# A planner that values work by its place in the run, and a second layer's setup that it can see

## Chip, cores and metric

The kernel runs on one core of one Trainium2 chip. The metric is the device time of one execution in microseconds; before the change it is 4598.14 us, the median of three runs (4592.67 to 4598.62).

## What is computed

Two layers over an fp32 tensor of 8 images, 192 channels, 64 x 64 pixels. Weights are fp32 throughout.

```python
# layer 0: windowed attention that keeps 16 keys, then an MLP
shortcut = layer_norm(xs); q, k, v = windows(shortcut) @ qkv_w.T          # 8x8 windows, 6 heads of 32
attn = l2n(q) @ l2n(k).T * temperature
attn = where(attn >= top_k(attn, 16)[..., -1:], attn, -100)
x2 = shortcut + proj(softmax(attn + rpb) @ v)
x  = x2 + fc2(gelu(fc1(layer_norm(x2))))
# layer 1: a filter in frequency space, then an MLP
xf = fft2(layer_norm(x) * n1_g + n1_b)                                    # over the 64 x 64 image
x  = x + ifft2(fc2(gelu(fc1([xf.real, xf.imag])))).real                   # 2 -> 16 -> 2
out = x + mlp2(gelu(mlp1(layer_norm(x))))                                 # 192 -> 768 -> 192
```

## The kernel before, in words

**Tiling.** Layer 0 works on bands of 8 rows (512 pixels): 8 bands an image, 64 in all. For each band, `front` transposes, normalizes and forms q, k and v; `attention` runs twice (once for each half of the windows); `back` projects, adds and runs the first MLP. Layer 1's filter works on groups of 16 channels: 12 groups an image, 96 in all. For each group, `forward` makes the first half of the transform (tiles `xf`, `fa`, `fz`), `pointwise` runs twice with its GELU (`fh`, `fo`), and `inverse` transforms back (`fb`, `fy`). It can begin when all 8 bands of an image have left layer 0. `leave` then runs the second MLP for each band, when all 12 groups of the image are done. In tile names, `_b` is the first MLP and `_d` the second: `mh_b`, `mh_d` are the products ahead of the GELU, `mo_b`, `mo_d` those behind it. `s` and `po` are attention's scores and its sums over values. From the second image on, attention weights go through DRAM to be turned (`tt`, `ar`, `at`, in `turned_by_dma`), and so do the MLPs' inputs (`lt`, `lr`, `hn`).

**Order.** Nothing in the order is written by hand, and no scheduler runs on the chip. Every task is a Python generator, and before each group of instructions it yields `op(engine, weight, ...)`: the engine, the time in units of 10 ns (the half of an MLP's second product has weight 390 and takes 3.90 us), the buffers it takes (`get`) and gives back (`put`), and what it waits for (`after`). `Plan.run` plays these through a model with five engine clocks. On each engine it takes, of the ops that could begin within 15 units, the one with the smallest key; the key is the begin time plus the task's `place` (360 units an image) plus noise. `Plan.search` (line 278) advances by 2000 units at a time: it tries 80 random noises to a horizon of 4000 units, rates each by the PE work in it plus 0.15 of the other engines' work, and keeps the first 2000 units of the best. `issue` then emits the instructions in that order, so each engine's queue has exactly the planned sequence. Semaphores hold the data dependences; a queue never overtakes.

**Modes.** TensorE's ops carry a mode name: `full` for 128-row products, `row64`, `row32`, `col32`, `s` and `v` for smaller arrangements of the array. The model charges 19 units for a change of mode on PE and 140 for a change of function on ACT (`CHANGE`, line 35).

**Buffers and arrivals.** `ARRIVES` (line 36) says how long after its end an op's result is seen by another engine: 28 units for PE, 18 for DVE, 15 for ACT, 11 for POOL, 265 for a DMA issued by SP. A buffer given back is free 150 units after an SP op and 15 after any other (line 268).

**Layer 1's setup.** `setup_layer1` (line 606) loads tables and weights through SP after the first attention half of band 0, in an op with no weight, so the plan sees no time on SP for it. The scale vector `n1g` comes through eight transfers whose source steps by four elements:

```python
src = bass.AP(n1t.tensor, n1t.offset + c * 2 * HC + k, [[0, 32], [4, 24], [1, 1]])
dst = n1g[32 * k : 32 * k + 32, 24 * c : 24 * c + 24]
nc.sync.dma_start(dst.unsqueeze(2), src)
```

Its DVE part waits for `("att", 0, 1, 1)`. `setup_mlp(1, ...)` (products `pf`, DVE scaling of `wmlp`) waits for `("att", 0, 5, 1)`.

Of the kernel before, what the change touches and what calls it, by code (L numbers as in the profile page):

```python
# [2 lines left out]

# [6 lines left out]
FP = mybir.dt.float32  # L10
# [6 lines left out]
C = 192  # L17
CA = 128
HC = 96
# [10 lines left out]
def op(engine, weight, mode=None, get="", put="", after=None, done=None, put_too=""):  # L30
    engines = ((engine, weight),) if isinstance(engine, str) else tuple(zip(engine, weight))
    return engines, mode, get.split(), (put + " " + put_too).split(), after, done
# [97 lines left out]
class Plan:  # L130
# [84 lines left out]
    def run(self, until, noise=None):  # L215
        ops, clock, mode, units = self.ops, self.clock, self.mode, self.units
        at, front, place, ready = self.at, self.front, self.place, self.ready
        while ready:
            found = {}
            for task, (number, begins) in ready.items():  # L220
                a = front[task]
                if a is not None and at[a] <= at[task]:
                    continue
                _, kind, counts, put, _, _ = ops[number]
                free = 0
                for name, n in counts:
                    u = units[name]
                    if len(u) < n:
                        break
                    if u[n - 1] > free:  # L230
                        free = u[n - 1]
                else:
                    best = None
                    for engine, weight, begin in begins:
                        if clock[engine] > begin:
                            begin = clock[engine]
                        if free > begin:
                            begin = free
                        change = kind and mode[engine] and kind != mode[engine]
                        cost = CHANGE[engine] if change else 0  # L240
                        end = begin + cost + weight + (40 if engine == "dve" else 0)
                        if best is None or end < best[0]:
                            best = end, engine, begin, cost, weight
                    _, engine, begin, cost, weight = best
                    key = begin + cost + place[task] - (100 if "ps" in put else 0)
                    if noise:
                        key += noise(number)
                    found.setdefault(engine, []).append((key, task, begin, cost, weight, number))
            if not found:
                return False  # L250
            chosen = None
            for engine, entries in found.items():
                first = min(e[2] + e[3] for e in entries) + 15
                e = min(e for e in entries if e[2] <= first)
                if chosen is None or (e[2], e[0]) < chosen[0]:
                    chosen = (e[2], e[0]), engine, e
            _, engine, (_, task, begin, cost, weight, number) = chosen
            if begin >= until:
                return True
            _, kind, counts, put, _, _ = ops[number]  # L260
            for name, n in counts:
                del units[name][:n]
            begin += cost
            end = begin + weight
            clock[engine] = end
            mode[engine] = kind or mode[engine]
            for name in put:
                units[name].append(end + (150 if engine == "sp" else 15))
                units[name].sort()
            self.end[number], self.engine[number] = end, engine  # L270
            self.log.append((number, task, engine, begin, weight))
            del ready[task]
            for other in self.blocked.pop(number, ()):
                self.wake(other)
            self.step(task)
        return True

    def search(self, tries=80, step=2000, horizon=4000, spread=25):
        draw = random.Random(1)
        now = 0  # L280
        while self.ready:
            now = max(now, self.clock["pe"])
            kept, best = self.save(), None
            for k in range(tries):
                seed = draw.random()
                noise = drawn(seed, spread) if k else None
                if not self.run(now + horizon, noise):
                    self.restore(kept)
                    continue
                worth = 0  # L290
                for _, _, engine, begin, weight in self.log[kept[-1]:]:
                    part = min(weight, max(0, now + horizon - begin))
                    worth += part if engine == "pe" else 0.15 * part
                if not self.ready:
                    worth = 1e9 - max(self.clock.values())
                if best is None or worth > best[0]:
                    best = worth, seed if k else None
                self.restore(kept)
            seed = best[1]
            self.run(now + step, drawn(seed, spread) if seed is not None else None)  # L300
            now += step
        return [(self.names[task], engine, number) for number, task, engine, _, _ in self.log]


def drawn(seed, spread):
    draw, values = random.Random(seed), {}

    def noise(number):
        if number not in values:
            values[number] = draw.gauss(0, spread)  # L310
        return values[number]

    return noise
# [28 lines left out]
def program(ctx, tc, x, out, w):  # L342
    nc = tc.nc
# [114 lines left out]
    def load_mlp(name1, name2):  # L458
        w1, w2 = load_ab(name1, DFF), ctile(name2, [128, 6, 64 + C])
        nc.sync.dma_start(w2[:, :, 64:], w[name2].rearrange("(c p) f -> p c f", p=128))  # L460
        return w1, w2
# [107 lines left out]
    def setup_mlp(layer, weights, gain, offset, after):  # L569
        yield op("pe", 120, "full", get="ps", after=after)  # L570
        w1, w2 = weights()
        pf = psum(f"pf_{layer}")
        for f in range(6):
            times(pf[:, 0, f : f + 1], w1, slice(f * 128, f * 128 + 128), offset)
        yield op("dve", 30, put="ps")
        nc.vector.tensor_tensor(fcb[:, layer], fcb[:, layer], pf[:, 0, 0:6], ALU.add)
        for k in range(2):
            yield op("dve", 64)
            scale(w1[k : k + 1], gain[k : k + 1])
        yield op("dve", 45, done=("mlp", layer))  # L580
        nc.vector.tensor_copy(w2[:, :, 0:64], w2[:, :, C:])
# [22 lines left out]
    wmlp = []  # L604

    def setup_layer1():
        yield op("pool", 0, get="xf", after=[("att", 0, 0, 1)])
        for j, name in enumerate(("fcos", "fsin")):
            nc.sync.dma_start(
                fhalf[:, j], w[name].rearrange("p (c u) -> p c u", c=2)[:, :, 0:U]  # L610
# [1 line left out]
            for e in range(2):  # L612
                own = w[name][64 * e : 64 * e + 64]
                for c in range(2):
                    rows = 64 * c + 32 * e
                    nc.sync.dma_start(ihalf[j][rows : rows + 32], own[0:32])

        for t in range(4):
            row = 64 * (t % 2) + 32
            nc.sync.dma_start(ihalf[1][32 * t : 32 * t + 1], w["fcos"][row : row + 1])  # L620
        for k in range(4):
            src = w["fwd2"].rearrange("(a b k e) v -> k b a e v", a=2, k=4, e=2)[k]
            nc.sync.dma_start(frow[8 * k : 8 * k + 8], src)
        for c in range(1, 4):
            nc.sync.dma_start(frow[32 * c : 32 * c + 32], frow[0:32])
        inv1 = sb.tile([128, 128], FP, tag="xf", name="inv1", bufs=1)
        nc.sync.dma_start(inv1, w["inv1"])
        sel1 = load("sel1", [128, 2, 8])
        sel2 = load("sel2", [128, 2, 16])
        aw1 = load("aw1", [128, 16])  # L630
        aw2 = load("aw2", [128, 2])
        nc.sync.dma_start(ab, w["ab"])
        n1t = w["n1"]
        for c in range(2):
            for k in range(4):
                src = bass.AP(
                    n1t.tensor, n1t.offset + c * 2 * HC + k, [[0, 32], [4, 24], [1, 1]]
                )
                dst = n1g[32 * k : 32 * k + 32, 24 * c : 24 * c + 24]
                nc.sync.dma_start(dst.unsqueeze(2), src)  # L640
            nc.sync.dma_start(n1b2[:, c, :], w["n1"][c : c + 1, 1, :])
        yield op("dve", 120, after=[("att", 0, 1, 1)])
        for e in range(2):
            for a in range(2):
                of = inv1[:, a * HW : (a + 1) * HW].rearrange("p (b k e) -> p e k b", k=4, e=2)
# [26 lines left out]
        yield op("dve", 50, done="layer1")  # L672
        nc.vector.tensor_scalar(dc, ab[0:1, 1:2], float(HW), None, ALU.mult)
        nc.vector.tensor_scalar(n1b2, n1b2, float(HW), None, ALU.mult)
        wmlp.extend(load_mlp("wmlp1", "wmlp2"))


# [784 lines left out]
    def leave(b, j):  # L1462
# [49 lines left out]
        ([(setup_rpb(), -0.1)], 1),  # L1512
        ([(setup_mlp(0, lambda: (wfc1, wfc2), vec(G2), vec(B2), ["rows", (None, 3000)]), -0.5)], 1),
        ([(setup_layer1(), 0.2)], 1),
        ([(setup_mlp(1, lambda: wmlp, *layer1, ["layer1", ("att", 0, 5, 1)]), 0.2)], 1),
        ([(front(b, i), at_band(b, i, -.12)) for b, i in bands], 1),
        ([(attention(b, i, hb), at_band(b, i, -.085)) for b, i in bands for hb in range(2)], 3),
        ([(back(b, i), at_band(b, i, .215)) for b, i in bands], 2),
# [86 lines left out]
```

## Time and profile before

| | |
|---|---|
| median of three runs | 4598.14 us |
| the profiled execution: its own time, and its span | 4606.84 us, 4605.0 us |
| TensorE clock granted, mean | 0.984 |
| busy: PE, its weight loads, DVE, ACT, POOL | 4377.8, 3470.0, 2769.9, 2506.5, 2337.6 us |
| PE idle, from 0 to 400 us | 67.7 us |
| PE idle, from 400 to 4300 us | 129.9 us |
| PE idle, from 4300 us to the end | 29.7 us |

The idle times are 100 us less PE's busy time in each stretch of 100 us, summed. A busy engine in this profile is one that has an instruction in flight: the ends of matmuls are modelled, and a change of mode is inside PE's busy time, not in its idle time.

### The profile page before, as it was taken

Reading aid. Unit: us, or ns where it says so; the run is one execution under the profiler, and the core shown is the slowest. Engines: PE = TensorE matmul, PEld = TensorE weight load, DVE = VectorE, ACT = ScalarE, POOL = GpSimd, SP = SyncE. Lnnn points to the kernel's source line nnn. Section 1 sums busy time; section 2 is a strip of 40 time slices with the busy share of each in tenths; the row PEclk is TensorE's granted clock in tenths of the full one; section 3 lists DMA queues with packets and bytes.
Section 4 is the critical chain, followed back from the end, with each engine's and each line's share of the span. In section 5 each row is a group of like instructions: output and inputs, shape, how many; then the busy total and the mean of one; then the engine's idle time right before and its main releaser. Section 6 shows DMA issues by size and latency. Waiting matters only on the chain. (4 is left out here: it accounts for less than half of the span.)

```text
span 4605.0 us, 143865 instructions
## 1 busy us (share of the span) xinstructions
PE 4377.8 (95%) x60506; PEld 3470.0 (75%) x60506; DVE 2769.9 (60%) x11070; ACT 2506.5 (54%) x3693; POOL 2337.6 (51%) x2161
## 2 busy tenths in 40 slices
PE   7888999999999999999999999999999999999989
PEld 5777777887778777778767877778777787778758
DVE  7888776746774466763767456774576744742111
ACT  4555666545663456544656446564566544653552
POOL 7787765525564365652756246663375533631100
PEclk8999999999999999999999999999999999999999
DMA  2001221311123111221122211222112221111002
GB/s 55 16 12 50 57 60 41 98 52 43 50 57 94 49 47 47 67 73 50 47 56 63 71 50 54 57 64 71 56 47 57 74 63 43 47 47 52 19 19 66
DMA packets 271072, 246.42 MB, mean 54 GB/s; under 512 B 39983, under 2 KB 223482, under 8 KB 270426
## 3 DMA queue, kind: packets, MB, share of 16 engines
q1 hardware_dynamic: 270414, 237.22, 18.6%
q8 instruction: 476, 7.80, 0.7%
q14 instruction: 170, 1.39, 0.1%
q10 hardware_dynamic: 12, 0.00, 0.0%
HBM read 120.52 MB, written 116.39 MB: 51 GB/s over the span
## 5 line engine op out<-in xcount | busy, mean ns | idle before, releaser
L1349 ACT ACTIVATE fh<-fh,ab 128x1024 f32<-128x1024 f32 x768 | 814.1, 1113 | 374.3 <-PE fh L1366 372.0
L960 POOL TENSOR_TENSOR nrm<-nrm,mhalf 128x24 f32<-128x24 f32 x128 | 549.0, 4289 | 10.7
L853 PE MATMUL mo_b<-wfc,h_b 128*128 128x192 f32 x3072 | 529.1, 330 | 1.2 <-ACT fh L1349 1.0
L853 PE MATMUL mo_d<-wmlp,h_d 128*128 128x192 f32 x3072 | 514.2, 327 | 2.7 <-ACT h_d L791 2.6
L853 PEld LDWEIGHTS mo_b<-wfc,h_b 128*128 128x128 f32 x3072 | 502.4, 191 | 14.3 <-issue 6.9
L853 PEld LDWEIGHTS mo_d<-wmlp,h_d 128*128 128x128 f32 x3072 | 498.6, 190 | 11.3 <-ACT h_d L791 4.8
L1153 POOL TENSOR_TENSOR s<-s,top 128x768 f32<-128x768 f32 x128 | 193.7, 1514 | 602.9 <-DVE s L1150 452.3
L1366 PE MATMUL fh<-fz,w1p 32*128 32x264 f32 (+1 forms) x6144 | 454.5, 401 | 10.8 <-issue 2.9
L791 ACT ACTIVATE h_d<-mh_d,fcb 128x512 f32<-128x512 f32 x384 | 241.0, 686 | 286.3 <-PE mh_d L820 221.7
L1366 PEld LDWEIGHTS fh<-fz,w1p 32*128 32x128 f32 x6144 | 288.0, 184 | 144.0 <-issue 79.6
L1393 PE MATMUL fo<-fh,w2p 128*32 128x248 f32 (+1 forms) x6144 | 384.3, 385 | 9.3 <-issue 3.8
L807 PE MATMUL mh_b<-hn_b,wfc_a 128*128 128x256 f32 x1536 | 375.6, 390 | 15.7 <-DMA hn_b<-lr_b 5.7
L807 PE MATMUL mh_d<-hn_d,wmlp_a 128*128 128x256 f32 x1536 | 363.0, 386 | 18.8 <-DMA hn_d<-lr_d 16.8
L807 PEld LDWEIGHTS mh_d<-hn_d,wmlp_a 128*128 128x128 f32 x1536 | 284.5, 190 | 79.9 <-issue 39.4
L807 PEld LDWEIGHTS mh_b<-hn_b,wfc_a 128*128 128x128 f32 x1536 | 279.5, 190 | 85.2 <-issue 30.1
L1143 DVE MATCH_REPLACE8 s<-top,s 128x64 f32<-128x64 f32 x1536 | 309.8, 209 | 0.0
L1393 PEld LDWEIGHTS fo<-fh,w2p 128*32 128x32 f32 x6144 | 188.6, 110 | 154.1 <-issue 29.4
L1479 DVE TENSOR_TENSOR zt<-mo_d,xy 128x768 f32<-128x768 f32 x64 | 61.0, 952 | 396.9 <-PE mo_d L853 396.5
L1163 POOL TENSOR_TENSOR s<-s,rsum 128x768 f32<-128x768 f32 x128 | 192.6, 1508 | 207.3 <-DVE rsum L1161 159.2
L791 ACT ACTIVATE h_b<-mh_b,fcb 128x512 f32<-128x512 f32 x384 | 239.5, 692 | 86.5 <-PE mh_b L820 72.3
L1141 DVE MAX8 top<-s 128x8 f32<-128x64 f32 x1536 | 256.9, 209 | 42.1 <-ACT s L1041 41.3
L702 POOL TENSOR_SCALAR rs_d<-mv_d 128x4 f32<-128x4 f32 x64 | 14.6, 229 | 526.2 <-DVE mv_d L695 504.0
(213 smaller groups left out, 8716.9 us busy)
## 6 DMA issues: line engine op xcount, KB each, us to landing
ar<-tt SPq DMA_DIRECT2D x448, 96.0 KB
at<-ar SPq DMA_DIRECT2D x112, 384.0 KB
lr_d<-lt_d SPq DMA_DIRECT2D x256, 96.0 KB
lr_b<-lt_b SPq DMA_DIRECT2D x224, 96.0 KB
xin<-in_x SPq DMA_DIRECT2D x64, 256.0 KB
hn_d<-lr_d SPq DMA_DIRECT2D x64, 256.0 KB
out<-z SPq DMA_DIRECT2D x64, 256.0 KB
hn_b<-lr_b SPq DMA_DIRECT2D x56, 256.0 KB
```

What stands on the lines that cost most here:

```text
L791: nc.scalar.activation(to, of, AF.Gelu, bias=fc1_bias[:, 2 * fp + k : 2 * fp + k + 1],)
L807: nc.tensor.matmul(ph[:, t, k * HALF : (k + 1) * HALF], w1[0][:, f], hn[:, t * HALF : (t + 1) * HALF], start=(first and k == 0), stop=not ...
L853: nc.tensor.matmul(acc[:, j, t * C : (t + 1) * C], hs[f // 2][:, f % 2, q * 128 : (q + 1) * 128], w2[:, f, ORDER[t]], start=(f == 0 and t ...
L960: nc.gpsimd.tensor_tensor(nf, nf, mhalf[:, :24], ALU.pow)
L1141: nc.vector.max(best[:, 0:8], of)
L1143: nc.vector.match_replace(s2, best[:, 0:8], of, -3.0e38)
L1153: nc.gpsimd.tensor_tensor(s, s, top[:, :, :, 0:1].to_broadcast(shape), ALU.subtract)
L1163: nc.gpsimd.tensor_tensor(s, s, row(rsum), ALU.mult)
L1349: nc.scalar.activation(hs[hf, k], ph, AF.Gelu, bias=ab[:, 0:1])
L1366: nc.tensor.matmul(phs[k // 2][:, k % 2, cols], w1p[i][rows, hf].rearrange("p h v -> p (h v)"), fz[rows, :] if rhs is None else zu[rows, : ...
L1393: nc.tensor.matmul(po[rows, :] if i == 0 else pou[rows, :, 1 : U - 1], w2p[i][:, hf].rearrange("p a v -> p (a v)"), hs[hf, k // 2][:, k % ...
L1479: nc.vector.tensor_tensor(zt.rearrange("p j (t c) -> p j t c", t=2), acc[:, :, : 2 * C].rearrange("p j (t c) -> p j t c", t=2), xy[:, :, : ...
```

## The change

1. **Work counts by its place.** `search` keeps count of the PE work done. `course()` lists the places in order with the PE work up to each, and so gives `here`, the place that the run has reached. Each task's work in the horizon is multiplied by exp(2 (here - place) / 360): a task one image behind counts 7.4 times one that is level. The other engines' work counts 0.05 instead of 0.15. There are 100 tries instead of 80, and where no try gets through, the search goes back three steps.
2. **Buffers** given back are free after `ARRIVES`, as results are: SP 265 instead of 150 units, PE 28, DVE 18 and POOL 11 instead of 15.
3. **Setup transfers planned.** `setup_layer1`'s transfers are SP ops with weights of 180 to 420 units. The load of `wmlp` is an SP op of its own, and `setup_mlp(1)` waits only for it. The DVE part of the setup waits for the transfers and no longer for an attention half.
4. **One vector as whole rows.** Two transfers broadcast rows of 96 elements of `n1` to 128 partitions, into a widened tile that `inv1` shares, and four DVE copies pick every fourth element into `n1g`.

```diff
             for name in put:
-                units[name].append(end + (150 if engine == "sp" else 15))
+                units[name].append(end + (150 if engine == "sp" else ARRIVES[engine]))
...
-    def search(self, tries=80, step=2000, horizon=4000, spread=25):
+    def search(self, tries=100, step=2000, horizon=4000, spread=25, mu=2.0, wt=0.05):
...
+            done += sum(v[4] for v in self.log[counted:] if v[2] == "pe")
+            counted = len(self.log)
+            here = course[bisect.bisect(course, (done,))][1] if done < course[-1][0] else course[-1][1]
+            value = [math.exp(mu * (here - place) / 360) for place in self.place]
...
-                for _, _, engine, begin, weight in self.log[kept[-1]:]:
-                    part = min(weight, max(0, now + horizon - begin))
-                    worth += part if engine == "pe" else 0.15 * part
+                    for _, task, engine, begin, weight in self.log[kept[-1]:]:
+                        part = min(weight, max(0, now + horizon - begin)) * value[task]
+                        worth += part if engine == "pe" else wt * part
...
     def setup_layer1():
-        yield op("pool", 0, get="xf", after=[("att", 0, 0, 1)])
+        yield op("sp", 420, get="xf", after=[("att", 0, 0, 1)])
...
-        inv1 = sb.tile([128, 128], FP, tag="xf", name="inv1", bufs=1)
+        first = sb.tile([128, 128 + C], FP, tag="xf", name="first", bufs=1)
+        inv1, gains = first[:, 0:128], first[:, 128:]
...
-            for k in range(4):
-                src = bass.AP(
-                    n1t.tensor, n1t.offset + c * 2 * HC + k, [[0, 32], [4, 24], [1, 1]]
-                )
-                dst = n1g[32 * k : 32 * k + 32, 24 * c : 24 * c + 24]
-                nc.sync.dma_start(dst.unsqueeze(2), src)
+            of = w["n1"][c, 0, :].partition_broadcast(128)
+            nc.sync.dma_start(gains[:, c * HC : (c + 1) * HC], of)
             nc.sync.dma_start(n1b2[:, c, :], w["n1"][c : c + 1, 1, :])
-        yield op("dve", 120, after=[("att", 0, 1, 1)])
+        yield op("dve", 60, after=[last])
+        for k in range(4):
+            rows = slice(32 * k, 32 * k + 32)
+            of = gains[rows].rearrange("p (n k) -> p k n", k=4)[:, k]
+            nc.vector.tensor_copy(n1g[rows], of)
+        yield op("dve", 120)
...
+        yield op("sp", 200, done="wmlp")
         wmlp.extend(load_mlp("wmlp1", "wmlp2"))
...
-        ([(setup_mlp(1, lambda: wmlp, *layer1, ["layer1", ("att", 0, 5, 1)]), 0.2)], 1),
+        ([(setup_mlp(1, lambda: wmlp, *layer1, ["wmlp"]), 0.2)], 1),
```

More of the change, by code (lines that the diff above doesn't have):

```diff
@@ L1 @@
+import bisect
+import math
 import random
@@ L276, in run @@
         return True
-    def search(self, tries=80, step=2000, horizon=4000, spread=25):
+    def search(self, tries=100, step=2000, horizon=4000, spread=25, mu=2.0, wt=0.05):
         draw = random.Random(1)
-        now = 0
+        now = done = counted = 0
+        course = self.course()
+        history = []
         while self.ready:
             now = max(now, self.clock["pe"])
+            done += sum(v[4] for v in self.log[counted:] if v[2] == "pe")
+            counted = len(self.log)
+            here = course[bisect.bisect(course, (done,))][1] if done < course[-1][0] else course[-1][1]
+            value = [math.exp(mu * (here - place) / 360) for place in self.place]
@@ L283, in search @@
             kept, best = self.save(), None
             for k in range(tries):
[L285 to L290, printed above, removed]
-                for _, _, engine, begin, weight in self.log[kept[-1]:]:
-                    part = min(weight, max(0, now + horizon - begin))
-                    worth += part if engine == "pe" else 0.15 * part
@@ L294, in search @@
[L294 to L297, printed above, removed]
-                self.restore(kept)
-            seed = best[1]
-            self.run(now + step, drawn(seed, spread) if seed is not None else None)
+                seed = draw.random() if k else None
+                if self.run(now + horizon, seed and drawn(seed, spread)):
+                    worth = 0
+                    for _, task, engine, begin, weight in self.log[kept[-1]:]:
+                        part = min(weight, max(0, now + horizon - begin)) * value[task]
+                        worth += part if engine == "pe" else wt * part
+                    if not self.ready:
+                        worth = 1e9 - max(self.clock.values())
+                    if best is None or worth > best[0]:
+                        best = worth, seed
@@ L301, in search, with course @@
+                self.restore(kept)
+            if best is None:
+                kept, now, done, counted = history[-min(3, len(history))]
+                del history[-3:]
+                self.restore(kept)
+                continue
+            history.append((kept, now, done, counted))
+            self.run(now + step, best[1] and drawn(best[1], spread))
             now += step
         return [(self.names[task], engine, number) for number, task, engine, _, _ in self.log]
+    def course(self):
+        work = []
+        for place, numbers in zip(self.place, self.lists):
+            engines = [self.ops[number][0][0] for number in numbers]
+            work.append((place, sum(weight for engine, weight in engines if engine == "pe")))
+        course, total = [], 0
+        for place, weight in sorted(work):
+            total += weight
+            course.append((total, place))
+        return course
@@ L616, in setup_layer1 @@
                     nc.sync.dma_start(ihalf[j][rows : rows + 32], own[0:32])
+        yield op("sp", 280)
         for t in range(4):
@@ L623, in setup_layer1 @@
             nc.sync.dma_start(frow[8 * k : 8 * k + 8], src)
+        yield op("sp", 180)
         for c in range(1, 4):
             nc.sync.dma_start(frow[32 * c : 32 * c + 32], frow[0:32])
-        inv1 = sb.tile([128, 128], FP, tag="xf", name="inv1", bufs=1)
+        yield op("sp", 280)
+        first = sb.tile([128, 128 + C], FP, tag="xf", name="first", bufs=1)
+        inv1, gains = first[:, 0:128], first[:, 128:]
         nc.sync.dma_start(inv1, w["inv1"])
@@ L632, in setup_layer1 @@
         nc.sync.dma_start(ab, w["ab"])
-        n1t = w["n1"]
+        last = yield op("sp", 180)
         for c in range(2):
-            for k in range(4):
-                src = bass.AP(
-                    n1t.tensor, n1t.offset + c * 2 * HC + k, [[0, 32], [4, 24], [1, 1]]
-                )
-                dst = n1g[32 * k : 32 * k + 32, 24 * c : 24 * c + 24]
-                nc.sync.dma_start(dst.unsqueeze(2), src)
-            nc.sync.dma_start(n1b2[:, c, :], w["n1"][c : c + 1, 1, :])
-        yield op("dve", 120, after=[("att", 0, 1, 1)])
+            of = w["n1"][c, 0, :].partition_broadcast(128)
+            nc.sync.dma_start(gains[:, c * HC : (c + 1) * HC], of)
+            nc.sync.dma_start(n1b2[:, c, :], w["n1"][c : c + 1, 1, :])
+        yield op("dve", 60, after=[last])
[4 more added lines that the diff above has]
+        yield op("dve", 120)
         for e in range(2):
```

## The prediction

> **What bounds the kernel now.** I began with the page's busy times and its 40 slices.
>
> ```profile
> PE 4377.8 (95%) x60506; PEld 3470.0 (75%) x60506; DVE 2769.9 (60%) x11070; ACT 2506.5 (54%) x3693; POOL 2337.6 (51%) x2161
> ...
> PE   7888999999999999999999999999999999999989
> ...
> DVE  7888776746774466763767456774576744742111
> ```
>
> TensorE is the bound: 227.2 us of the span are left beside it, and a better order can only take from those, or from what PE spends on the order itself. Stretches of 100 us (columns: time, PE, PEld, DVE, ACT, POOL, clock, DMA share, GB/s) place the idle time: 67.7 us before 400 us, 29.7 us after 4300 us, 129.9 us between.
>
> ```profile
> 1200.00:1300.00 100.00, 92.96 (x1734) 67.98 (x1730) 77.93 (x303) 64.40 (x84) 64.22 (x53) 0.97 0.22 62
> ...
> 2100.00:2200.00 100.00, 98.15 (x1146) 79.34 (x1146) 32.04 (x111) 47.09 (x65) 28.54 (x28) 0.98 0.14 37
> ...
> 4400.00:4500.00 100.00, 81.58 (x1218) 61.01 (x1212) 18.33 (x66) 41.62 (x56) 7.06 (x16) 0.91 0.11 29
> ```
>
> In the middle PE idles where DVE is loaded. Of the 38 stretches from 400 to 4200 us, the 12 with DVE over 72% lose 4.8 us each, the 9 from 65 to 72% 4.1, the 12 under 55% 1.7. The PE waits of 400 to 4300 us (total, times, longest) are scattered; only the first is large:
>
> ```profile
> PE po L1186 <- DMA at<-ar: 29.0, 22, 2.7
> PE fa L1296 <- POOL xf L1290: 6.8, 8, 1.8
> ...
> PE fh L1366 <- DVE fz L1331: 1.8, 1, 1.8
> ```
>
> Last, the chain in order of time (start, length, what), for the price of a change of array mode:
>
> ```profile
> 4067.88 1.93 PE mh_b L820 x16
> 4069.80 1.92 PE mh_b L807 x8
> ...
> 4207.74 7.80 PE mo_d L853 x48
> ...
> 4230.21 8.00 PE mo_d L853 x48
> ...
> 4513.23 1.73 PE mh_d L807 x8
> ```
>
> The same 8 products take 1.92 us behind 64-row products (L820) and 1.73 us behind `mo_d`, which has their own mode. The same 48 take 8.00 us behind the 32-row `fz`, 7.80 us behind the 128-row `fa` (the PE timeline shows what precedes). So a change of mode costs **0.19 to 0.20 us**, inside PE's busy time.
>
> **What the Trainium skill says.** "TensorEngine Tiling (Array Packing)", section Key Properties: a change of tiling mode drains TensorE. The 0.19 us above agree. "ScalarE: Activation LUTs", section What ACT_TABLE_LOAD costs: 1283 ns for every load, whatever the set; the trace's mean is 1283 ns too. "DMA: Bandwidth & Descriptors", in its table of cases: a last dimension that is not contiguous becomes one descriptor per element. That fits the eight `n1g` loads of 3 KB each (columns: start, length, issue):
>
> ```profile
> 73.10 6.10 SPq L640 DMA_DIRECT2D n1g<-in_n  x4
> 79.24 1.52 SPq L641 DMA_DIRECT2D n1b<-in_n  x1
> 80.80 16.05 SPq L640 DMA_DIRECT2D n1g<-in_n  x4
> 96.90 0.38 SPq L641 DMA_DIRECT2D n1b<-in_n  x1
> 97.38 2.72 SPq L381 DMA_DIRECT2D xin<-in_x  x1
> 100.15 8.02 SPq L384 DMA_DIRECT2D xin<-in_x  x2
> ```
>
> **Part by part.** I compared the two programs' instruction orders, engine by engine. To place things I priced every PE product by its family's mean in the profile of before (busy time over number) and scaled the sum to PE's 4378 us: "PE work" below is that ruler.
>
> *The setup.* 22.2 us of issues for `n1g` go, and the 10.7 us in which the band load behind them (`xin`) crept out become the 1.4 us of its neighbours; two row transfers (about 0.6 us each, as other issues) and four DVE copies of 32x48 (about 0.2 us each, as a 128x32 copy there) come. The op that opens the setup sat on POOL's queue without an instruction, so its move to SP takes nothing from POOL. SP gains about 30 us at 73 to 108 us, but no PE wait there names one of these transfers: worth 0 on the path. What covers it is that band 5's data are needed at about 170 us (SP then reloads their buffer), and `n1g` at 396 us.
>
> The setup moves, too. The 24 products `pf` of the second MLP ran at 256 to 262 us; in the new order they are PE row 173 instead of 432, directly behind `mo_b` of band 0, so at about 105 us. Their weights load behind `xin` of band 5, which needs band 3's transposes (86 to 87 us); before, load and weights kept the DMA engines busy for 11 us, from 109 to 120. So weights at about 100 us against a use at 105: worth 0, and if they came as late as before, PE would stand for up to 15 us with its whole queue behind it. The DVE part of the setup (row 197 instead of 275) is the same work earlier; the first 320 us are DVE's anyway. The first 269 products on PE and the last 180 instructions on ACT are the same in both programs, so I leave the 67.7 us at the head (within 3 us) and the 29.7 us at the tail as they are.
>
> *Modes.* Giving each PE product its mode, I count 2043 changes in the old order and 1952 in the new: 91 fewer, at 0.19 us = **-17 us**. All of it is on PE, so on the path. Bounds: 0.10 us (the difference of the timeline's own durations, where the chain's step also includes the later start) gives -9, and 0.30 gives -27. ACT's table loads fall from 202 to 190, 12 x 1.283 = 15 us of ACT, which is busy 54%: nothing by itself.
>
> *Attention's cover.* Between a half band's last scores `s` and its `po` lie DVE's top-16, POOL, the softmax and the DRAM turn. The PE work planned between them is under 30 us for 17 of 112 half bands before, and for 10 after; that is where the 22 waits of 1.3 us (29.0 us) come from. 7 x 1.3 = **-9 us**. From both sides: all 29 go, or the waits stay (0); a gain of both is possible since DMA releases are now planned 1.15 us later (265 against 150 units).
>
> *Evenness.* Work is spread differently: counted in stretches of 100 us of PE work from 400 to 4000, those in which attention's products exceed 6 us fall from 9 to 5, and those under 3 us from 8 to 3. The idle of the stretches against DVE load is nearly straight, so evening out gains little: 0 by the straight line, -8 by a parabola through the 38 points. I take **-4**.
>
> *Layer 1's cover.* In return the group chain gets tighter: its groups start later (`fa` of image 1 from 773 to 885 us of PE work) and end earlier (1257 to 1186). Pairs with little PE work between them rise: `fa` to `fz` under 3 us from 11 to 19, `fz` to `fh` under 3 from 3 to 9, `fo` to `fb` under 2 from 62 to 72, of 96 each. Before, all 76 such pairs together cost about 4 us of waits (`fz` on `fa` 1.0, `fh` on `fz` 1.8, `fb` on `fo` 0.5), so 24 more cost **+1**; at the longest wait seen there, 1.8 us, they cost 43.
>
> Sum: -17 - 9 - 4 + 1 = -29, call it **-30 us** with the head's few. The profiled execution took 4606.84 us, so a profiled 4577; that is 8.7 us above the median shown, 4598.14, and the forecast against the median is **4568 us**, 0.65% less.
>
> **Rivals.**
>
> A, the sum above: 4568. With drains at 0.30 us, attention's cover midway to 29 us and the parabola it is -27 - 19 - 8 + 1 = -53, so 4545; with drains at 0.10 us and nothing else, 4590.
>
> B, slower: the tighter group chain. Each `fz`, `fa` or `fo` result that comes late stops PE at the head of its queue, while attention and MLP products that could run stand behind. For it: DVE also carries attention in these stretches, and the counts above all rise. Against: such pairs cost next to nothing before. At 1.8 us for 24 pairs it is 43 us; it decides from 1.3 us each (above 30 us), and with the attention waits unimproved it gives 4598 - 17 - 4 + 43 = 4620.
>
> C, no change: matmul ends in the profile are modelled, so the price of a drain may be the model's, and the idle may only move from `po` to the group chain: 4590 to 4606, say 4598. Every group of waits but one being under 7 us speaks for it.
>
> D, much faster: half of the middle's 130 us are plan errors (buffers believed free too early), and the new arrivals mend them: 4598 - 17 - 65 = 4516. Against: waits that name a DMA are only about 38 us there.
>
> E, the early `pf` stands for its weights: 15 us back, 4583.
>
> **How the numbers follow.** A 0.50, D 0.16, E 0.05, C 0.13, B 0.16. A measurement of this kernel can tell about 0.2%, 9 us, from no change. Faster by more than that: A, D and E and a little of C, 0.73. Within: 0.11. Slower: B, 0.16. A alone reaches from 4545 to 4590; with half of D and half of B, 8 in 10 lie between 4530 and 4612.
>
> **What would show it.** Right: PE's busy time down by 10 to 25 us with the same number of matmuls; waits of `po` for `at<-ar` at some 20 us; idle from 400 to 4300 us at 110 to 125; the head within 3 us of 67.7 and the tail near 29.7; table loads 190; no `n1g` transfers; `pf` near 105 us without a wait. Wrong: PE busy unchanged although 91 changes of mode went (the price), waits of `fz`, `fh` or `fb` above 15 us together (B), a wait of `pf` for `wmlp` (E), or a head that differs by more than 5 us.

## The result, and the profile after

The changed kernel takes 4571.18 us (median of five runs, 4564.65 to 4582.48), against 4598.14 us: a ratio of 0.9945, 95% interval 0.9928 to 0.9962. The forecast was 4568. The profiled execution took 4572.44 us with a span of 4570.6, 34.4 us less than the span before. The page's busy times and slices:

```profile
PE 4352.8 (95%) x60506; PEld 3469.2 (76%) x60506; DVE 2753.7 (60%) x11035; ACT 2510.7 (55%) x3725; POOL 2333.0 (51%) x2156
...
PE   7888999999999999999999999999999999999989
...
DVE  7777677646575566656657656766567656742111
```

The same 60506 matmuls keep PE busy 25.0 us less, and its idle time falls from 227.2 to 217.8 us, by 9.4: together the 34.4. DVE's row is the visible change. Before, 3s and 4s stood beside 7s between the head and the tail; now nearly all digits there are 5 to 7. In stretches of 100 us from 400 to 4200 us, DVE's busy share scatters by 10.7 points (standard deviation) instead of 13.3, around the same mean (62.6 before, 62.7 now); stretches over 72% fall from 12 to 8. Three stretches (time, PE, PEld, DVE, ACT, POOL, clock, DMA share, GB/s):

```profile
1200.00:1300.00 100.00, 96.86 (x1750) 69.45 (x1748) 60.07 (x229) 69.00 (x98) 57.52 (x51) 1.00 0.21 57
...
1800.00:1900.00 100.00, 91.24 (x1284) 72.75 (x1282) 71.76 (x276) 52.84 (x82) 56.96 (x57) 0.95 0.25 69
...
2100.00:2200.00 100.00, 97.04 (x1565) 75.16 (x1558) 54.31 (x200) 52.10 (x68) 38.98 (x37) 0.98 0.12 31
```

At 1200 us DVE has come down from 78 to 60% and PE lost 3.1 us instead of 7.0; at 2100 us DVE has gone up from 32 to 54% and PE lost 3.0 instead of 1.9. The worst stretches of the middle are now the first, from 400 us (9.6 us lost), and the one at 1800 us (8.8). Idle from 400 to 4200 us: 113.7 us, 129.9 before. The head has 71.8 (67.7 before), the last 305 us have 32.2 (29.7). PE's waits from 400 to 4300 us (total, times, longest):

```profile
PE po L1214 <- DMA at<-ar: 25.8, 23, 2.5
PE fb L1452 <- issue: 10.8, 10, 1.7
PE mh_d L835 <- DMA hn_d<-lr_d: 10.1, 4, 8.1
PE fa L1324 <- POOL xf L1318: 8.2, 7, 3.1
```

The first wait has hardly moved, and there are two more of it before 400 us (2.7 us). The 8.1 us of the third is one wait, for a transfer, and makes up nearly all of the loss at 1800 us: that stretch does not show what DVE's load costs. The setup as SP issues it (start, length, issue):

```profile
71.94 0.43 SPq L662 DMA_DIRECT2D first<-in_n  x1
72.41 0.29 SPq L663 DMA_DIRECT2D n1b<-in_n  x1
72.74 0.34 SPq L662 DMA_DIRECT2D first<-in_n  x1
73.13 0.28 SPq L663 DMA_DIRECT2D n1b<-in_n  x1
89.26 0.33 SPq L404 DMA_DIRECT2D xin<-in_x  x1
...
90.84 0.58 SPq L452 DMA_DIRECT2D wmlp_a<-in_wmlp  x1
```

The vector costs SP 0.8 us in place of 22.2 (the page counts 5984 fewer packets under 512 B, 33999 for 39983; the eight old loads held 8 x 768 = 6144 elements), band 5's load goes out when its buffer is free, and the weights of the second MLP follow 17 us earlier than before. The products `pf` start at 105.9 us and do not wait.

### The profile page after: what moved, and what is told of

Read it like the earlier page. It is cut to its first block, busy times and chain, and to the rows that moved or that the text cites. A ratio compares the mean times of both kernels' runs of the same rounds, so it can differ in the third digit from the quotient of the medians.

```text
span 4570.6 us, 143923 instructions
## 1 busy us (share of the span) xinstructions
PE 4352.8 (95%) x60506; PEld 3469.2 (76%) x60506; DVE 2753.7 (60%) x11035; ACT 2510.7 (55%) x3725; POOL 2333.0 (51%) x2156
## 2 busy tenths in 40 slices
DMA packets 265088, 246.49 MB, mean 54 GB/s; under 512 B 33999, under 2 KB 217498, under 8 KB 264442
## 4 chain that ended last, share of the span: by engine, by line
PE 42%; POOL 6%; DVE 6%; ACT 2%; DMA 2%; issue 1%; SPq 1%; ACTq 0%; DVEq 0%; POOLq 0%
PE mo_d L881 7%; PE mh_d L835 5%; PE mo_b L881 4%; PE fh L1394 4%; PE fo L1421 3%; POOL nrm L988 3%; PE mh_b L835 3%; PE mh_d L848 3%; PE mh_b L848 1%; PE pq L1004 1%; PE fa L1324 1%; PE fy L1469 1%; DMA at<-ar 1%; PE fz L1349 1%; PE po L1214 1%
## 5 line engine op out<-in xcount | busy, mean ns | idle before, releaser
L988 POOL TENSOR_TENSOR nrm<-nrm,mhalf 128x24 f32<-128x24 f32 x128 | 556.9, 4351 | 10.7
L1421 PE MATMUL fo<-fh,w2p 128*32 128x264 f32 (+1 forms) x6144 | 379.8, 383 | 5.1 <-ACT fh L1377 2.8
L1169 DVE MAX8 top<-s 128x8 f32<-128x64 f32 x1536 | 256.2, 208 | 50.7 <-ACT s L1069 50.2
L1173 DVE MAX8 top<-s 128x8 f32<-128x64 f32 x1536 | 265.3, 214 | 0.0
L1126 DVE TENSOR_TENSOR qk<-qk,nrm 128x768 f32<-128x768 f32 x102 | 137.2, 1345 | 202.6 <-POOL nrm L989 202.4
```

The source lines that it names most:

```text
L988: nc.gpsimd.tensor_tensor(nf, nf, mhalf[:, :24], ALU.pow)
L1169: nc.vector.max(best[:, 0:8], of)
L1173: nc.vector.max(best[:, 8:16], s2)
L1421: nc.tensor.matmul(po[rows, :] if i == 0 else pou[rows, :, 1 : U - 1], w2p[i][:, hf].rearrange("p a v -> p (a v)"), hs[hf, k // 2][:, k % ...
```

## The experiments

Twelve kernels. Each was compared with the kernel before on its own chip, so ratios to it are compared with each other. "Idle" below is PE's idle time from 400 to 4200 us in the profiled execution, "scatter" DVE's standard deviation over the same 38 stretches in points, "changes" the array's changes of mode counted in the order. Small differences of idle time mean nothing: the changed kernel's order, emitted again with small edits, gave 110.3 (e1) and 113.2 us (e11) beside its 113.7.

| kernel | place in the value | changes | PE busy, us | idle, us | scatter | ratio to before (95%) |
|---|---|---|---|---|---|---|
| before | no | 2043 | 4377.8 | 129.9 | 13.3 | 1 |
| before, draw 2 (e5) | no | 2037 | 4394.2 | 155.4 | 16.6 | 1.0134 (1.0119 to 1.0149) |
| before, draw 3 (e7) | no | 2070 | 4383.5 | 131.1 | 16.1 | 1.0053 (1.0036 to 1.0071) |
| before with new setup (e4) | no | 2034 | 4387.1 | 142.9 | 16.0 | 1.0076 (1.0060 to 1.0093) |
| after without place (e2) | no | 2048 | 4392.8 | 158.7 | 17.0 | 1.0133 (1.0118 to 1.0148) |
| the same, weight 0.05 (e9) | no | 2016 | 4372.3 | 129.2 | 12.1 | 1.0046 (1.0037 to 1.0056) |
| after | yes | 1952 | 4352.8 | 113.7 | 10.7 | 0.9945 (0.9928 to 0.9962) |
| after, draw 2 (e6) | yes | 1975 | 4349.9 | 115.1 | 10.5 | 0.9926 (0.9906 to 0.9946) |
| after, draw 3 (e8) | yes | 1967 | 4336.5 | 110.6 | 11.0 | 0.9903 (0.9886 to 0.9921) |
| before with new search (e3) | yes | 1942 | 4336.9 | 119.5 | 10.9 | 0.9936 (0.9916 to 0.9957) |
| after, weight 0.15 (e10) | yes | 2020 | 4347.0 | 110.7 | 10.2 | 0.9909 (0.9890 to 0.9929) |
| after, 300 tries (e12) | yes | 1912 | 4329.7 | 92.1 | 11.8 | 0.9819 (0.9799 to 0.9839) |

### e1: more changes of mode in the same plan

```diff
+                if fp == 1 and not isinstance(nc, Mute):
+                    product = halves[n][2]
```

> The changed kernel with its plan kept as it is; only where the instructions are emitted, the middle third of each MLP's first product does its two halves in the opposite order, so that the array changes its mode 2171 times instead of 1952 (219 more). Every product stays. If a change of mode costs TensorE 0.19 us (the theory of the prediction): PE busy time up by 42 us, from 4353 to about 4395, and the time up by 35 to 45 us, to about 4610. If the price is only the profile's modelling of matmul ends (rival C): the time within 10 us of 4571, whatever PE's busy time says.

Measured: 4603.80 us, ratio 1.0018 (1.0011 to 1.0024); over the changed kernel's 0.9945 that is 1.0073, or 33 us (22 to 44 if the ends of both intervals are set against each other), just below the 35 to 45 that I expected. PE busy 4392.4, 39.6 us up: 0.18 us for each of 219. The chain of the changed kernel near its end, where one band follows another (start, length):

```profile
4504.54 8.00 PE mo_d L881 x48
...
4516.85 3.65 PE mh_d L835 x16
...
4521.56 8.00 PE mo_d L881 x48
```

and of this one:

```profile
4520.34 8.00 PE mo_d L883 x48
...
4531.78 1.92 PE mh_d L835 x8
...
4534.77 1.92 PE mh_d L835 x8
...
4537.76 8.00 PE mo_d L883 x48
```

A band takes 17.02 us in the first (4521.56 - 4504.54) and 17.42 us in the second, with two more changes of mode in each: 0.20 us for one, read from starts and not from modelled ends. Both 128-row groups now come behind 64-row ones and take 1.92 us each, where the pair took 3.65. So the price is no product of modelled ends: the same products take longer with more changes, and rival C's doubt about it falls.

### e5 to e8: other random numbers

```diff
-        draw = random.Random(1)
+        draw = random.Random(2)
```

(3 in e7 and e8; in the kernel before for e5 and e7, in the changed one for e6 and e8.)

> The kernel before with the search's random numbers started from 2 instead of 1; nothing else. It changes mode 2037 times (2043 before). If a plan's time hardly depends on the draw: 4588 to 4606, as before. If the draw decides as much as the change does (so that the measured gain may be luck): a spread of 20 us or more around it.

> The changed kernel with random numbers started from 2. It changes mode 1975 times (1952). If the gain belongs to the rating by place: 4560 to 4585, below the kernel before with the same start. If it was luck of the draw: anywhere between 4560 and 4630.

> The kernel before with random numbers started from 3: 2070 changes of mode. Little dependence on the draw: 4590 to 4610 (27 more changes of mode are 5 us). Luck of the draw: off by 20 us or more.

> The changed kernel with random numbers started from 3: 1967 changes of mode. If the gain belongs to the rating: 4560 to 4585, at least 15 us below the kernel before with the same start. Luck of the draw: no such order.

Measured: 4662.01 and 4624.64 us for the old search, 4566.47 and 4557.61 us for the new one. I had not expected the first two. With the old rating, three draws lie between 4598 and 4662, so **the kernel before was the best of its three draws**; with the new one they lie between 4558 and 4571. Draw for draw the new kernel is faster by 0.55, 2.1 and 1.5%, 1.4% in the mean of the three. The measured 0.55% is the smallest. The page of the worst old draw (e5):

```profile
PE 4394.2 (94%) x60506; PEld 3477.6 (75%) x60506; DVE 2775.5 (60%) x11058; ACT 2488.1 (53%) x3689; POOL 2346.4 (50%) x2171
...
PE   6888999999999999999999999999999999999989
...
DVE  6878777627775476744676447773576734832111
```

DVE swings between 2 and 8 there: 17 of the 38 stretches have it over 72%, and these lose 5.4 us of PE each.

### e2, e3, e4: the parts one by one

```diff
# e2, in the changed kernel
-    def search(self, tries=100, step=2000, horizon=4000, spread=25, mu=2.0, wt=0.05):
+    def search(self, tries=100, step=2000, horizon=4000, spread=25, mu=0.0, wt=0.15):
# e3: the kernel before with search() and course() of the changed kernel, nothing else
# e4: the changed kernel with the search and the buffer times of the kernel before
-                units[name].append(end + (150 if engine == "sp" else ARRIVES[engine]))
+                units[name].append(end + (150 if engine == "sp" else 15))
```

> The changed kernel with the place taken out of the value of work (mu 0) and the other engines' work at 0.15 again; 100 tries, the new buffer times and the new setup stay. It changes mode 2048 times, as often as the kernel before (2043). If the gain comes with the rating of work by place: about 4598, PE busy about 4375. If it comes from the new buffer times or the setup: about 4571.

> The kernel before with the new search alone (place in the value, weight 0.05, 100 tries); old buffer times, old setup transfers. It changes mode 1942 times, with 166 table loads. If the rating by place carries the gain: 4565 to 4580, PE busy about 4355. If buffer times and setup carry it: about 4598.

> The kernel before with the new setup alone (planned transfers, rows of the vector, the early setup products); old search and old buffer times. It changes mode 2034 times. The prediction's working says the setup is worth nothing on the path: 4590 to 4606. If the setup is what gained: about 4575.

Measured: 4655.52, 4568.90 and 4632.21 us. The new search alone (e3) brings all of the gain; taking the place and the low weight out of its rating (e2) loses it and more. Both times without it lie above the 4598 that I expected, e4 by 36 us against the kernel before on its chip (0.76%). By itself that would say that the setup is harmful. Beside e5 and e7 it says no more than another draw of the old search: any edit to the tasks gives another plan. The new buffer times show no gain that stands out either: e2 has them, with the new setup and 100 tries, and is among the slow ones. They were not tried alone.

### e9, e10: which of the two weights

```diff
# e9, then e10, in the changed kernel
-    def search(self, tries=100, step=2000, horizon=4000, spread=25, mu=2.0, wt=0.05):
+    def search(self, tries=100, step=2000, horizon=4000, spread=25, mu=0.0, wt=0.05):
...
+    def search(self, tries=100, step=2000, horizon=4000, spread=25, mu=2.0, wt=0.15):
```

> The changed kernel with the place taken out of the value (mu 0) but the other engines' work still at 0.05. It changes mode 2016 times, and attention's share of PE work by stretches of 100 us scatters by 1.52 us (1.62 before, 1.11 changed). If the place is what evens the load: like the old plans, DVE's load by stretches scattering by 13 or more points, 130 to 160 us of idle PE between 400 and 4200 us, 4600 to 4650. If the lower weight is what gained: about 4570.

> The changed kernel with the place in the value (mu 2) and the other engines' work back at 0.15. Attention's share scatters by 1.04 us, even less than in the changed kernel (1.11), but the array changes its mode 2020 times, almost as often as before. This parts the two causes. If evenness sets the idle time: DVE scatter near 10.5 points, 110 to 120 us of idle PE between 400 and 4200 us. The 61 more changes of mode than the mean of the new plans (1959) cost 12 us at 0.19: about 4577. If fewer changes of mode carry all of the gain: about 4595 or above, with as much idle time as the old plans.

Measured: 4617.85 and 4555.82 us. The place decides; the low weight is not needed. The six plans of the table with the place in the value lie between 0.9819 and 0.9945, the six without it between 1 and 1.0134. e10 also parts the two mechanisms, since its order is even but changes mode nearly as often as the old ones:

```profile
PE 4347.0 (95%) x60506; PEld 3453.6 (76%) x60506; DVE 2755.8 (61%) x11026; ACT 2508.0 (55%) x3721; POOL 2351.3 (52%) x2173
```

Its idle time is 110.7 us with a scatter of 10.2, as expected. So the idle time does not follow the changes of mode. That it follows the evenness is not shown: e10 has the place in its value too, and among the plans without it e9, the kernel before and e7 have 129 to 131 us idle at scatters of 12.1, 13.3 and 16.1. e10's time came out 21 us below the 4577 that I had expected: PE was busy less, not more, than in the changed kernel. Part of that may be the clock: granted 0.9865 in the mean over the span, 0.9831 in the changed kernel. Taking (1 - clock) x span off the busy time, as an estimate of the busy time at the full clock, leaves 4285 us here, 4275 there: 10 us more for 68 more changes. In e9, with 2016 changes, 4302 us are left: 17 us more than in e10 for as many changes. e9 fits the old plans in its time, with less scatter (12.1) than the 13 that I expected and an idle time of 129.2 us.

### e11: the old transfers in the new plan

```diff
-            of = w["n1"][c, 0, :].partition_broadcast(128)
-            nc.sync.dma_start(gains[:, c * HC : (c + 1) * HC], of)
+            for k in range(4):
+                src = bass.AP(
+                    n1t.tensor, n1t.offset + c * 2 * HC + k, [[0, 32], [4, 24], [1, 1]]
+                )
+                dst = n1g[32 * k : 32 * k + 32, 24 * c : 24 * c + 24]
+                nc.sync.dma_start(dst.unsqueeze(2), src)
...
-        for k in range(4):
-            rows = slice(32 * k, 32 * k + 32)
-            of = gains[rows].rearrange("p (n k) -> p k n", k=4)[:, k]
-            nc.vector.tensor_copy(n1g[rows], of)
```

> The changed kernel with its plan kept as it is; only where the instructions are emitted, the vector comes through the eight transfers of the kernel before, and the four DVE copies are left out. If the prediction is right that the rows are worth nothing: within 9 us of 4571. Against it: the weights of the second MLP now stand behind these transfers on SP; if they come some 10 us late for the products planned at 106 us, TensorE waits there and the time is up by 5 to 15 us.

Measured: 4581.56 us, ratio 0.9970 (0.9960 to 0.9981), about 11 us above the changed kernel's 0.9945; the intervals just meet, and the two profiled spans are equal (4570.5 and 4570.6; that execution was the fastest of e11's eleven), so the sum is not settled. What happens at the place is plain. SP:

```profile
80.37 17.46 SPq L667 DMA_DIRECT2D n1g<-in_n  x4
...
98.36 3.61 SPq L404 DMA_DIRECT2D xin<-in_x  x1
...
106.73 0.82 SPq L452 DMA_DIRECT2D wmlp_a<-in_wmlp  x1
```

PE:

```profile
114.98 0.56 PE L507 MATMUL pf<-va,wmlp_a 128*128 128x1 f32 x2 [4.55 <-DMA wmlp_a<-in_wmlp]
116.06 0.58 PE L507 MATMUL pf<-vb,wmlp_b 64*128 64x1 f32 x2 [0.53 <-DMA wmlp_b<-in_wmlp]
```

and the stretches around it (PE first, the clock after POOL):

```profile
110.00:115.00 5.00, 0.45 (x38) 0.34 (x18) 1.36 (x9) 0.86 (x2) 1.93 (x4) 0.57 0.97 218
115.00:122.00 7.00, 6.47 (x26) 6.22 (x27) 0.18 (x2) 0.00 (x0) 0.00 (x0) 0.50 0.29 67
```

PE is busy 0.45 of 5 us while the weights arrive at 218 GB/s, and then runs the 24 products at half clock: they end at 121.8 us instead of 110.5. This is rival E. The row transfers keep it away; the head's idle time is 77.6 us here and 71.8 with them. Nothing behind `pf` goes ahead meanwhile: all 60506 products stand in the same order in both traces, and up to 1570 us each starts 8 to 13 us later than in the changed kernel. After that the two come together again, to 0.2 us at the end; PE's mean clock was 0.9841 in this execution and 0.9831 in the other, which as (1 - clock) x span is 4.6 us of it.

### e12: more tries

```diff
-    def search(self, tries=100, step=2000, horizon=4000, spread=25, mu=2.0, wt=0.05):
+    def search(self, tries=300, step=2000, horizon=4000, spread=25, mu=2.0, wt=0.05):
```

> The changed kernel with 300 tries for each step of the search instead of 100. It changes mode 1912 times (1952), and attention's share scatters by 1.07 us (1.11). If changes of mode and evenness are what count: 40 x 0.19 = 8 us of PE less, about 4560. If the plans are at their limit or the model's ratings no longer match the chip: 4565 to 4580.

Measured: **4514.29 us**, ratio 0.9819 (0.9799 to 0.9839): faster than both kernels, by 1.8% than the one before. I had expected 4560.

```profile
PE 4329.7 (96%) x60506; PEld 3459.4 (77%) x60506; DVE 2756.1 (61%) x11058; ACT 2512.3 (56%) x3700; POOL 2337.5 (52%) x2166
...
PE   7998999999999999999999999999999999999989
...
DVE  7788766646775656674656757756567656652111
```

Against the changed kernel PE is busy 23.1 us less and idle 33.7 us less: 21.6 in the middle, 10.7 at the head (61.1). The scatter is 11.8, no lower, and 40 fewer changes of mode explain only 8 us. So evenness and changes of mode are not all of what a better plan has. One draw was tried, and the old rating was not given 300 tries: how much of this belongs to longer search with any rating is open.

## Why the prediction was right, and where not

The time was right, 4568 against 4571, and the likeliest case was the one that happened. Of its terms:

- *Modes, -17.* The price holds: 0.18 from PE's busy time, 0.20 from the band period in e1, 0.19 in the working. 91 changes are 16 to 18 us. PE's busy time fell by 25.0. The rest goes with the new plans, too: busy time less (1 - clock) x span is 4302 to 4310 us in the six plans without place and 4270 to 4281 in the four with place, weight 0.05 and 100 tries, 31 us between the means for 82 changes. The changes explain half of it; what the other half is stays open. Among the six plans with place alone the price comes out once more: from 4265 us at 1912 changes (e12) to 4285 at 2020 (e10), 0.19 us for each.
- *Attention's cover, -9.* **This step failed.** The half bands with less than 30 us of PE work between `s` and `po` did fall from 17 to 10, but the waits of `po` for `at` only went from 29.0 to 28.5 us with those before 400 us. The count was read as the cause of the waits and is not. In the traces (half bands keep their order, so the k-th `s` belongs to the k-th `po`) 19 half bands before and 10 after have less than 30 us of busy PE in between, and they hold only 6 of the 22 waits before (8.8 of 29.0 us) and 4 of the 25 after. Where `po` waited for `at`, it started 27 to 62 us behind its scores before and 27 to 49 after: a fixed cover of 30 us does not tell which half band waits. What makes that chain long or short, DVE's and POOL's queues or another thing, was not tested.
- *Evenness, -4.* The direction was right, the size too small. Idle in the middle fell by 16.2 us, 3.2 of it in the waits of `po` for `at`. I had taken the curve of idle time against DVE load within one plan, which is nearly straight, so that moving load gains nothing. Between plans the relation is another: scatter 10.2 to 11.0 goes with 111 to 120 us, 12.1 to 13.3 with about 130, 16.0 to 17.0 with 131 to 159. That it is the scatter itself, and not what else comes with the place in the value, no run shows; e12 (11.8 with 92 us) speaks against scatter alone. Nor does one wait carry the fall: those of `mh_b` shrank most, from 12.6 to 1.7 us, but e8 has 11.6 us of them and as little idle time.
- *Layer 1's cover, +1.* Right in size. PE's waits of `fa`, `fz`, `fh`, `fo`, `fb` and `fy` came to 41 us in the middle before and 38 after, although `fb` alone rose from 5 to 13. Rival B did not happen. Its sign, `fz`, `fh` and `fb` above 15 us together, was badly set: they come to 19.8 us after, but came to 19.7 before.
- *Setup, 0.* Right for the time, with the cover as stated: weights ready before `pf` at 105.9 us. But what covers it is the fourth part of the change. The transfers I costed at nothing in the old order cost the products `pf` 11 us at their place in the new one, and as much in the medians, where it is less sure (e11).
- *Head and tail, 0.* The head rose by 4.1 us, one more than allowed for, and the stretch from 400 to 500 us lost 9.6 us instead of 4.2; the tail's last 305 us rose by 2.5.
- *Rival D* saw plan errors mended by the new buffer times. e2 has those times and is as slow as any plan. The 4514 us of e12 came with more tries and no other change.

So the sum was right partly by luck, because terms made up for each other: of attention's -9 only 3.2 us came in the middle and next to nothing in all, head and tail took 6.6 us back, and in return PE's busy time fell by 8 us more than was priced, and the idle time of the middle outside those waits by 13.0 us where 3 were priced. Two of the signs set for a right forecast did not come either: waits of `po` for `at` of some 20 us, and a head within 3 us. What the prediction never asked is how the *kernel before* stood among the plans of its own search. It was the best of three draws, and the mean gain over the three is about 60 us.

## What to carry to other kernels

Where a planner or a search with random draws writes the order, run two or three draws of both versions before a difference is put down to the edit: here the old search's own spread of 64 us was more than twice the gain, and one part (e4) looked harmful by 36 us, which is within that spread. A rating that values work by its place, and not only the bound engine's occupancy in a window, gave six plans here that were all faster than the six without it and had DVE's load more even (scatter 10.2 to 11.8, against 12.1 to 17.0). Where changes of array mode are frequent, count them in the order: at 0.2 us each, 2000 of them are 9% of this run.

## What the hardware showed that I had not expected

A clock of 0.50 makes products longer inside PE's busy time, and a wait need not stand before it. In e11 TensorE stood 4.55 us for weights, and the 24 products behind took 6.8 us (114.98 to 121.8) instead of 4.6 (105.9 to 110.5), at a clock of 0.50. That looks as if the wait had cost more than its length. But in the changed kernel, where PE was busy without a gap from 90 to 110 us and `pf` waited for nothing, the clock fell at nearly the same time, in the middle of `pf` (stretches, then two pairs of products):

```profile
100.00:105.00 5.00, 5.00 (x33) 4.96 (x31) 3.50 (x9) 0.42 (x1) 4.84 (x4) 1.00 0.02 3
...
110.00:115.00 5.00, 4.11 (x78) 3.63 (x78) 4.67 (x33) 2.22 (x5) 1.17 (x3) 0.50 0.02 3
```

```profile
108.08 0.38 PE L507 MATMUL pf<-vb,wmlp_b 64*128 64x1 f32 x2
108.39 0.59 PE L507 MATMUL pf<-va,wmlp_a 128*128 128x1 f32 x2
```

So the wait is not shown to be what lowered the clock in e11; the late products fell wholly into a time of 0.50, the early ones in part. Busy time holds such loss as well as changes of mode do, so that two plans with the same products can differ in PE's busy time by when these meet a low clock.
